# Seven stretches of a graph layer's gathers take 114 to 126 rows in place of 128

## The chip, the cores and the metric

The kernel runs on one core of one Trainium2 chip. The time is device microseconds of that core. Before the change it is 18006.2 us, the median of two runs (18000.0 and 18012.4).

## The reference, cut to what matters

A graph layer over 50,000 nodes with 160 features (64 scalars and 32 vectors of three) and 1,650,000 edges: 800,000 random pairs in both directions and a loop at each node, sorted by destination. Every edge takes its source node's features, combines them with its own four attributes, and the results are summed at the destination. Then come a linear map, a relu, two residual additions and a layer norm.

```python
dst = jnp.concatenate([_d, _s, _loop])
_o = jnp.argsort(dst, stable=True)
src, dst = src[_o], dst[_o]
...
ss, vv = (s[src], v[src])                       # gather per edge
dot = jnp.einsum('eui,ei->eu', vv, e1)
out0 = C0 * (ss * e0 @ W1 + dot * INV3 @ W2)
...                                             # p3, p4, p5 -> out1
m_agg = jax.ops.segment_sum(m, dst, num_segments=n)
h = ...                                         # m_agg times Ws and Wv
return x + jax.nn.relu(h)
...
x = _layernorm(x + ref(x, ...), axis=-1)
```

Everything up to the relu is linear in the source features, so the kernel sums first and multiplies by the weights afterwards: per node, for each of the four attributes, the sum over its edges of attribute times source row.

## The kernel before, in words

Edges are taken in the order of their destination. 128 of them, one per partition, make a unit; six units (G) make a group, twenty groups (SG) a chunk of 120 units. A group's 768 edges reach few nodes, so its sums fit a window of 32 node slots (W).

For a unit, POOL issues one indirect DMA (L398) that fetches 128 rows of x, 640 bytes each, into a slice of the tile `xg`. A tile holds two groups (PG), so twelve gathers, and there are four such tiles; a gather into a tile waits until the matmuls on its earlier contents are done. DVE builds the other operand: `hot` (L419) marks each edge's node slot, and `ha` (L422) multiplies the marks with the four attributes, giving 128 columns (4 attributes times 32 slots). PE multiplies `ha` with the gathered rows (L447) and sums a group's six units in PSUM; each matmul waits for its own gather's semaphore. DVE then transposes the sums (L462) and adds them into a ring of nodes (L471), at a position read from the data. When a block of 128 nodes is complete, PE multiplies it with the weights (L776), and DVE and ACT do the residual and norm (L184 to L200).

Loops of nodes aren't gathered: after a head of the first 100 groups (five chunks), which reads the inputs as they are, rows of edges are packed by DVE and stored to memory without the loops (`edges`, L683), 11 times 128 rows of 1185 edges, and the later chunks read these. The nodes' own rows come in through `xr`. A chunk's edges are loaded by SP (L267, and L273 for the first node of each group) and turned so that edge and unit change places.

The order of work on SP, PE, DVE and ACT is written out by hand: a loop over pairs of groups issues the gathers of a pair, its matmuls, and between these in small portions whatever is due (packing steps, blocks, loads). A chunk's load is asked for three pairs before the chunk ahead of it starts (LEAD), and turned one to two pairs after that start.

## Time and profile before

| | before |
|---|---|
| median of the runs | 18006.2 us |
| the profiled execution | 18022.0 us |
| its span | 18020.3 us |
| POOL busy | 11866.1 us (66%), 12,522 gathers among 12,535 instructions |
| DVE busy | 7478.3 us (41%) |
| PE busy, weight loads | 6860.2 us (38%), 6095.4 us (34%) |
| DMA | 1341.6 MB, mean 74 GB/s |
| TensorE clock granted | 0.627 |

Busy time is that of instructions as the profiler recorded them; for a gather on POOL it is the time in which the engine makes the transfer ready, not the transfer. Idle time is counted just before the instruction that follows it, with what ended it as far as semaphore events show. "issue" means that the engine waited for nothing that the profile shows, and "remote" that the releaser isn't known. q0 is the queue of the gathers, q1 that of SP.

### The profile page before, as it was taken

Reading aid. Unit: us, or ns where it says so; the run is one execution under the profiler, and the core shown is the slowest. Engines: PE = TensorE matmul, PEld = TensorE weight load, DVE = VectorE, ACT = ScalarE, POOL = GpSimd, SP = SyncE. Lnnn points to the kernel's source line nnn. Section 1 sums busy time; section 2 is a strip of 40 time slices with the busy share of each in tenths; the row PEclk is TensorE's granted clock in tenths of the full one; section 3 lists DMA queues with packets and bytes.
Section 4 is the critical chain, followed back from the end, with each engine's and each line's share of the span. In section 5 each row is a group of like instructions: output and inputs, shape, how many; then the busy total and the mean of one; then the engine's idle time right before and its main releaser. Section 6 shows DMA issues by size and latency. Waiting matters only on the chain. (4 is left out here: it accounts for less than half of the span.)

```text
span 18020.3 us, 93561 instructions
## 1 busy us (share of the span) xinstructions
PE 6860.2 (38%) x28971; PEld 6095.4 (34%) x28972; DVE 7478.3 (41%) x12038; ACT 171.6 (1%) x273; POOL 11866.1 (66%) x12535
## 2 busy tenths in 40 slices
PE   3333334333333333333333333333333333333433
PEld 2233333333333333333333333333333333333333
DVE  7344245334524442453344345434433452444232
ACT  0000000000000000000000000000000000000000
POOL 6566666666666666666666666666666666666666
PEclk6666666666666666666666666666666666666666
DMA  2222322322332233223223322332232233222222
GB/s 72 79 71 78 79 68 73 83 76 70 77 81 70 71 80 77 70 73 85 73 70 78 80 70 72 82 77 69 72 85 74 69 76 78 72 70 71 75 72 61
DMA packets 740962, 1341.57 MB, mean 74 GB/s; under 512 B 243310, under 2 KB 522674, under 8 KB 725894
## 3 DMA queue, kind: packets, MB, share of 16 engines
q0 software_dynamic: 601056, 1026.60, 23.5%
q1 hardware_dynamic: 138138, 308.06, 5.6%
q8 instruction: 231, 3.78, 0.1%
q14 instruction: 273, 2.24, 0.0%
q10 hardware_dynamic: 1264, 0.88, 0.0%
HBM read 1263.28 MB, written 71.42 MB: 74 GB/s over the span
## 5 line engine op out<-in xcount | busy, mean ns | idle before, releaser
L398 POOL DMA_INDIRECT xg<-in_x,si x12522 | 11862.6, 947 | 6108.8 <-issue 3663.5
L447 PE MATMUL ps<-xg,ha 128*128 128x160 f32 x25044 | 6282.8, 397 | 9643.7 <-issue 5600.4
L447 PEld LDWEIGHTS ps<-xg,ha 128*128 128x128 f32 x25044 | 5409.4, 267 | 10356.9 <-issue 10352.3
L462 DVE STREAM_TRANSPOSE sums<-ps 128x320 f32<-128x320 f32 x1044 | 527.0, 505 | 6249.8 <-remote 4712.4
L422 DVE TENSOR_TENSOR ha<-hot,pk 128x1536 f32<-128x1536 f32 x1044 | 1830.4, 1753 | 52.1 <-remote 11.0
L776 PE MATMUL phb<-BWk,ring 128*128 128x160 f32 (+1 forms) x3910 | 1176.4, 381 | 1441.0 <-issue 858.6
L184 DVE SCALAR_TENSOR_TENSOR y<-phb,xt 128x320 f32<-128x320 f32 x196 | 95.9, 489 | 3623.2 <-PE ps L447 2504.7
L776 PEld LDWEIGHTS phb<-BWk,ring 128*128 128x128 f32 (+1 forms) x3910 | 894.1, 258 | 1489.1 <-issue 886.9
L471 DVE TENSOR_TENSOR ring<-ring,sums 128x160 f32 x2087 | 684.5, 328 | 253.1 <-issue 158.6
L419 DVE TENSOR_TENSOR hot<-bank,rel 128x384 f32<-128x384 f32 x1044 | 570.6, 547 | 67.4 <-DMA xt<-in_x 67.3
L632 DVE COPY_PREDICATED prow<-marks,prow 128x2370 f32<-128x2370 int32 (+5 forms) x198 | 550.3, 2780 | 1.1
L766 DVE STREAM_TRANSPOSE ring<-xr 128x1280 f32<-128x1280 f32 x188 | 437.2, 2326 | 0.1
L632 DVE COPY_PREDICATED pra<-marks,pra 128x1580 f32<-128x1580 int32 (+5 forms) x198 | 378.8, 1913 | 0.0
L763 DVE TENSOR_TENSOR xr<-xr,bank 128x1280 f32<-128x1280 f32 x188 | 276.5, 1471 | 4.6 <-DVE bank L756 1.4
L194 ACT ACTIVATE rstd<-mv,eps_t 128x2 f32<-128x2 f32 x196 | 58.0, 296 | 16997.5 <-DVE mv L189 12612.7
L468 DVE TENSOR_TENSOR ring<-ring 128x196 f32<-128x196 f32 (+20 forms) x485 | 149.4, 374 | 1.8
L200 DVE TENSOR_SCALAR o<-y,mv,rstd 128x160 f32<-128x160 f32 x391 | 130.2, 374 | 10.9 <-remote 1.6
L629 DVE COPY_PREDICATED_SCALAR hit<-marks,none 128x395 int32 (+5 forms) x198 | 130.1, 657 | 10.9 <-DVE pri L627 3.2
L716 DVE MEMSET ring<- 128x1280 f32 (+1 forms) x98 | 119.3, 1218 | 23.1 <-issue 21.0
L188 DVE BATCH_NORM_STATS2 st<-y 128x6 f32<-128x160 f32 x391 | 121.7, 311 | 6.7
L630 DVE COPY_PREDICATED hit<-marks,pri 128x395 int32<-128x395 int32 (+5 forms) x198 | 118.5, 598 | 10.4 <-issue 2.2
L627 DVE TENSOR_TENSOR pri<-hit,marks 128x395 int32<-128x395 int32 (+11 forms) x198 | 113.5, 573 | 14.8 <-issue 3.2
(346 smaller groups left out, 1752.7 us busy)
## 6 DMA issues: line engine op xcount, KB each, us to landing
xg<-in_x,si POOLq DMA_INDIRECT x12522
xr<-in_x SPq DMA_DIRECT2D x93, 1280.0 KB
r<-edges SPq DMA_DIRECT2D x100, 384.0 KB
edges<-prow SPq DMA_DIRECT2D x1330, 27.8 KB
xt<-in_x SPq DMA_DIRECT2D x195, 160.0 KB
out<-o SPq DMA_DIRECT2D x195, 160.0 KB
pra<-in_attr SPq DMA_DIRECT2D x10, 2370.0 KB
selves<-mine SPq DMA_DIRECT2D x1328, 0.8 KB
```

Of the source, the lines that this page charges most:

```text
L200: nc.vector.tensor_scalar(o[:n, i], y[:n, i], mv[:n, i, 0:1], rstd[:n, i:i + 1], op0=ALU.subtract, op1=ALU.mult)
L398: part = nc.gpsimd.indirect_dma_start(out=xg[:, j, :], out_offset=None, in_=x, in_offset=bass.IndirectOffsetOnAxis(ap=placed[0][:, u + j:u ...
L419: idle[:] = [nc.vector.tensor_tensor(hot[:, :n], slotsP[:, 0:W].unsqueeze(1).to_broadcast([P, n, W]), rel[:, u:u + n].unsqueeze(2).to_broa ...
L422: nc.vector.tensor_tensor(ha[:, :n], hot[:, :n].unsqueeze(2).to_broadcast([P, n, NK, W]), pk[:, :, u:u + n].rearrange("p k u -> p u k").un ...
L447: mm = nc.tensor.matmul(ps[:, j // G, :], ha[:, j].rearrange("p k w -> p (k w)"), xr, start=j % G == 0, stop=j % G == G - 1)
L462: nc.vector.transpose(at[:, :ng], ps[:, :ng].rearrange("p g (b f) -> p g b f", f=FB))
L468: nc.vector.tensor_tensor(ring[k][:, b, :past], ring[k][:, b, :past], ring[k - 1][:, b, S:S + past], op=ALU.add)
L471: nc.vector.tensor_tensor(here, here, at[:, i], op=ALU.add)
L632: nc.vector.copy_predicated(what[:n, a:e], mi[:, r].unsqueeze(2).to_broadcast([n, e - a, what.shape[2]]), what[:n, a + d:e + d])
L763: nc.vector.tensor_tensor(xr[:, r], xr[:, r], sumP[:, r].unsqueeze(2).to_broadcast([P, r.stop - q, D]), op=ALU.mult)
L766: nc.vector.transpose(here[:, r], xr[:, r].rearrange("p q (b f) -> p q b f", f=FB))
L776: wrote("misc", nc.tensor.matmul(ph[:nb], ring[k][:, i, cols], BWk[:, i, :], start=i == 0, stop=i == ND - 1))
```

## The change

In seven stretches of eight chunks the gathers take fewer than 128 rows: 126 in chunks 8 to 15, 125 in 20 to 27, 124 in 32 to 39, 121 in 44 to 51, 119 in 56 to 63, 114 in 68 to 75 and 120 in 80 to 87. Between these and at the end stand chunks of 128, and the chunks before them, the head among them, are as they were. A unit then holds that many edges, on the first partitions; the operands of the matmul are cut to these partitions. With fewer edges in a unit there are more units: the number of groups goes from 2087 to 2146. What stands at which edge is now read from a list of starts, and the loads of a short chunk are split in two, one for the first 96 partitions (whole blocks of 32) and one for the last 32.

```diff
+SIZES = (126, 125, 124, 121, 119, 114, 120)
+
+def size_of(s):
+    i, j = divmod(s - 8, 12)
+    return SIZES[i] if 0 <= i < len(SIZES) and j < 8 else P
...
-    ngroups = math.ceil((n_edges - n_nodes + eh * n_nodes / n_edges + far) / (group * P))
+    starts = [0]
+    while starts[-1] < n_edges - n_nodes + eh * n_nodes / n_edges + far:
+        g = len(starts) - 1
+        starts.append(starts[-1] + group * (P if g < head else size_of(g // SG)))
...
     def near(g):
-        p = g * G * P
+        p = starts[g]
...
+                if size[s] < P:
+                    m = size[s] // W
+                    for i, what_ in ((slice(0, m), what[0:P * size[s] * c]), (slice(m, NK), what[m * W * c:])):
+                        by_unit = what_.rearrange("(u q) -> u q", u=P)[:, 0:(i.stop - i.start) * W * c]
+                        dq.dma_start(to[i.start * W:i.stop * W], by_unit.rearrange("u (i q) -> i u q", q=W * c))
+                    return
...
-            nc.vector.tensor_reduce(extremes[:, 0, s:s + 1], rel[:, :n], axis=AX.X, op=ALU.min)
+            nc.vector.tensor_reduce(extremes[:size[s], 0, s:s + 1], rel[:size[s], :n], axis=AX.X, op=ALU.min)
...
                 part = nc.gpsimd.indirect_dma_start(
-                    out=xg[:, j, :], out_offset=None, in_=x,
-                    in_offset=bass.IndirectOffsetOnAxis(ap=placed[0][:, u + j:u + j + 1], axis=0))
+                    out=xg[:size[s], j, :], out_offset=None, in_=x,
+                    in_offset=bass.IndirectOffsetOnAxis(ap=placed[0][:size[s], u + j:u + j + 1], axis=0))
...
-                mm = nc.tensor.matmul(ps[:, j // G, :], ha[:, j].rearrange("p k w -> p (k w)"), xr,
+                mm = nc.tensor.matmul(ps[:, j // G, :], ha[:xr.shape[0], j].rearrange("p k w -> p (k w)"), xr,
```

Also, `extremes` is set to zero once, and the list of places at which the program changes its margin for a group's first node (`cuts`) has the starts and ends of the stretches added.

The instructions of POOL, before, from the last ones ahead of the main loop to its end (`xg` are the gathered rows, the first number of a shape is the rows of one gather, and xN says how many stand in a row):

```order
L803 IOTA quarter 128x4
L999 IOTA place 128x1185
L398 DMA xg<-in_x,si 128x160 x49
L505 IOTA at 1x1408
L398 DMA xg<-in_x,si 128x160 x12473
L885 TENSOR_LOAD more
```

The same place now, from the same gathers to the stretch of 114 (the line of the gather is now L420):

```order
L420 DMA xg<-in_x,si 128x160 x911
L420 DMA xg<-in_x,si 126x160 x960
L420 DMA xg<-in_x,si 128x160 x480
L420 DMA xg<-in_x,si 125x160 x960
L420 DMA xg<-in_x,si 128x160 x480
L420 DMA xg<-in_x,si 124x160 x960
L420 DMA xg<-in_x,si 128x160 x480
L420 DMA xg<-in_x,si 121x160 x960
L420 DMA xg<-in_x,si 128x160 x480
L420 DMA xg<-in_x,si 119x160 x960
L420 DMA xg<-in_x,si 128x160 x480
L420 DMA xg<-in_x,si 114x160 x960
```

The 49 ahead of `at` are the same; behind these rows stand 480 of 128, 960 of 120 and 2316 of 128. So the queue holds 12,876 gathers, 354 more than before, and 6,720 of them are short.

SP's instructions before, around the load of chunk 8 (`fd` and `r` are a chunk's first nodes and edges, `xt` a block's rows of x, `sa` and `xr` shares and rows of the nodes themselves, `out` the result):

```order
L709 DMA xt<-in_x 128x320
L875 DMA out<-o 128x320
L273 DMA fd<-edges 128x1x1
L267 DMA r_4696<-edges 128x2x384
L709 DMA xt<-in_x 128x320
L746 DMA sa<-selves 128x1x64
L746 DMA xr<-in_x 128x1x2560
```

And now:

```order
L731 DMA xt<-in_x 128x320
L897 DMA out<-o 128x320
L295 DMA fd<-edges 128x1x1
L286 DMA r_4697<-edges 96x4x192
L286 DMA r_4697<-edges 32x4x192
L731 DMA xt<-in_x 128x320
L768 DMA sa<-selves 128x1x64
L768 DMA xr<-in_x 128x1x2560
```

One load has become two, with the next block's rows and the nodes' own rows behind them.

More of the change, by code (lines that the diff above doesn't have):

```diff
@@ L100, in plan @@
     rows = math.ceil((n_edges - eh) / row) + 2
-    ngroups = math.ceil((n_edges - n_nodes + eh * n_nodes / n_edges + far) / (group * P))
-    assert eh + (rows - 1) * row - n_nodes + eh * n_nodes / n_edges - far >= ngroups * group * P
+    starts = [0]
+    while starts[-1] < n_edges - n_nodes + eh * n_nodes / n_edges + far:
+        g = len(starts) - 1
+        starts.append(starts[-1] + group * (P if g < head else size_of(g // SG)))
+    assert size_of((len(starts) - 2) // SG) == P and len(starts) - 1 > head + SG
+    assert eh + (rows - 1) * row - n_nodes + eh * n_nodes / n_edges - far >= starts[-1]
     units = P * math.ceil(max(math.ceil(n_edges / P) + again - 1, math.ceil((eh + rows * row + 1) / P)) / P)
-    return nblk, nb, again, group, units, ngroups, row, head, rows, far
+    return nblk, nb, again, group, units, starts, row, head, rows, far
 @with_exitstack
@@ L110, in tile_gnn_resnorm @@
     N = x.shape[0]
-    NBLK, NB, GA, G, NU, NG, L, NH, NR, FAR = plan(N, n_edges)
+    NBLK, NB, GA, G, NU, starts, L, NH, NR, FAR = plan(N, n_edges)
+    NG = len(starts) - 1
     EH = NH * G * P
@@ L212, in tile_gnn_resnorm @@
     S = SB * P
-    cuts = sorted({0, NH, NG} | {round(i * NG / 10 / SG) * SG for i in range(10)})
+    cuts = sorted({0, NH, NG} | {round(i * NG / 10 / SG) * SG for i in range(10)}
+                  | {g for g in range(NH, NG, SG) if size_of(g // SG) != size_of(g // SG - 1)})
     parts = list(zip(cuts, cuts[1:]))
@@ L219, in tile_gnn_resnorm @@
     NSC = math.ceil(NG / SG)
+    size = [P if s * SG < NH else size_of(s) for s in range(NSC)]
     part_of = [next(i for i, (g0, g1) in enumerate(parts) if g0 <= s * SG < g1) for s in range(NSC)]
@@ L243, in tile_gnn_resnorm @@
         extremes = once.tile([P, 2, NSC], F32, name="extremes")
+        nc.vector.memset(extremes, 0.0)
         count_ = once.tile([1, SG], F32, name="count")
@@ L279, in load @@
                     at = (at[0], g0 - f0, ng)
-                p0, q0 = u0 * P - EH, f0 * G * P - EH
+                p0, q0 = (starts[g0] - EH + (u - g0 * G) * size[s] for u in (u0, f0 * G))
                 r6 = rawp.tile([P, NK * W * C], F32, name="r6").rearrange("p (b e c) -> p b e c", b=NK, c=C)
                 fd = rawp.tile([P, 1], F32, name="fd")
-                fetch_first(fd, edges[0, q0 * C + 1:(q0 + W * G * P) * C + 1], C)
-                fetch(r6.rearrange("p b e c -> p b (e c)"), edges[0, p0 * C:(p0 + P * P) * C], C)
+                fetch_first(fd, edges[0, q0 * C + 1:(q0 + W * G * size[s]) * C + 1], C)
+                fetch(r6.rearrange("p b e c -> p b (e c)"), edges[0, p0 * C:(p0 + P * size[s] + size[s] % P // W * W) * C], C)
                 return s, at, None, None, fd, r6[:, :, :, 0:2].rearrange("p b e c -> p c b e"), r6[:, :, :, 2:]
@@ L382, in place @@
                 op0=ALU.min, op1=ALU.subtract)
-            nc.vector.tensor_reduce(extremes[:, 0, s:s + 1], rel[:, :n], axis=AX.X, op=ALU.min)
-            begun.append(nc.vector.tensor_reduce(extremes[:, 1, s:s + 1], rel[:, :n], axis=AX.X, op=ALU.max))
+            nc.vector.tensor_reduce(extremes[:size[s], 0, s:s + 1], rel[:size[s], :n], axis=AX.X, op=ALU.min)
+            begun.append(nc.vector.tensor_reduce(extremes[:size[s], 1, s:s + 1], rel[:size[s], :n], axis=AX.X, op=ALU.max))
             placed[s] = si, rel, pk[:, :, us]
@@ L405, in gather @@
                 tc.add_to_no_dep_group(key, part.ins)
-                rows.append((xg[:, j, :], filled[t][j], 16 * gathers[t][j], key))
+                rows.append((xg[:size[s], j, :], filled[t][j], 16 * gathers[t][j], key))
             return rows
@@ L918, in reach @@
         def reach(s):
-            end = min(NG, (s + 1) * SG) * G * P
+            end = starts[min(NG, (s + 1) * SG)]
             if s * SG < NH:
@@ L923, in reach @@
             if s + 1 < NSC:
-                end = max(end, (s * SG * G + P) * P)
+                end = max(end, starts[s * SG] + P * size[s] + size[s] % P // W * W)
             if s * SG == NH:
-                end = max(end, (s * SG + W) * G * P)
+                end = max(end, starts[s * SG] + W * G * size[s])
             return end - EH
```

## The prediction

> **What bounds the kernel now.** I read the page first, by engines, queues and groups.

> ```profile
> span 18020.3 us, 93561 instructions
> PE 6860.2 (38%) x28971; PEld 6095.4 (34%) x28972; DVE 7478.3 (41%) x12038; ACT 171.6 (1%) x273; POOL 11866.1 (66%) x12535
> q0 software_dynamic: 601056, 1026.60, 23.5%
> q1 hardware_dynamic: 138138, 308.06, 5.6%
> L398 POOL DMA_INDIRECT xg<-in_x,si x12522 | 11862.6, 947 | 6108.8 <-issue 3663.5
> ```

> No engine is full. But the 12,522 gathers of L398 fill POOL end to end: 11862.6 us busy and 6108.8 us idle just before them make 17971.4 us, so 48.9 us of the span is left for everything else. One gather's slot is 17971.4 / 12522 = 1.435 us, and the time of this kernel is the number of gathers times their slot. The slot has three parts: 0.947 us busy, an issue gap, and waits. The view of waits splits the last two.

> ```profile
> POOL xg L398 <- issue: 3663.5, 12020, 1.7
> POOL xg L398 <- PE ps L447: 1220.3, 220, 33.2
> POOL xg L398 <- remote: 1201.7, 275, 6.9
> PE ps L447 <- issue: 5600.4, 2943, 24.0
> PE ps L447 <- DVE ha L422: 3280.4, 462, 61.0
> ```

> The issue gap is 3663.5 / 12020 = 0.305 us. The rest, 6108.8 - 3663.5 = 2445.3 us, is 0.195 us a gather, and stands in some 500 waits of several us. The timeline of POOL shows how they fall (these are its rows with a wait, from one answer):

> ```profile
> 5135.98 0.95 POOL L398 DMA_INDIRECT xg<-in_x,si  x1 [6.50 <-PE ps L447]
> 5170.51 0.94 POOL L398 DMA_INDIRECT xg<-in_x,si  x1 [4.74 <-PE ps L447]
> 5204.95 0.94 POOL L398 DMA_INDIRECT xg<-in_x,si  x1 [4.59 <-remote]
> 5239.69 0.94 POOL L398 DMA_INDIRECT xg<-in_x,si  x1 [5.03 <-remote]
> ```

> These waits are 34.5 us apart, which is 24 gathers (two tiles of twelve): 24 x 1.25 us of gathering and about 4.6 us of waiting for one of the four xg buffers, which PE's matmuls hand back. So POOL can issue at 1.25 us, and something downstream holds it to 1.435. The timeline of all engines up to the second of these waits shows PE then:

> ```profile
> 5164.82 0.94 POOL L398 DMA_INDIRECT xg<-in_x,si  x1 [0.30 <-issue]
> 5165.12 0.43 PE L447 MATMUL ps<-xg,ha 128*128 128x160 f32 x1 [2.37 <-issue]
> 5166.52 0.28 PEld L447 LDWEIGHTS ps<-xg,ha 128*128 128x128 f32 x1 [2.50 <-issue]
> 5167.92 0.42 PE L447 MATMUL ps<-xg,ha 128*128 128x160 f32 x1 [2.37 <-issue]
> 5170.02 1.30 PEld L447 LDWEIGHTS ps<-xg,ha 128*128 128x128 f32 x5 [1.12 <-issue]
> 5170.03 1.43 PE L447 MATMUL ps<-xg,ha 128*128 128x160 f32 x4 [0.27 <-issue]
> ```

> While gathers stream, PE gets one instruction every 1.40 us (5165.12, 5166.52, 5167.92) with no releaser that the profile names; some 4 us after POOL has stopped it runs four matmuls in 1.43 us. So gathers in flight slow PE, PE hands buffers back late, POOL waits, and that lets PE catch up. What in a gather does this (its 128 rows, its completion on the DMA engines, or its being one instruction) the trace doesn't show, since all its gathers are alike. It does show what it is not: the pace hardly moves with other traffic. Two stretches of the windows view (busy time of the gathers' own tile, granted clock, DMA share, GB/s):

> ```profile
> 5400.00:5850.00 450.00, 162.97 (x625) 139.21 (x626) 297.24 (x314) 0.63 0.28 70
> 13050.00:13500.00 450.00, 159.21 (x644) 137.29 (x644) 293.75 (x312) 0.62 0.32 84
> ```

> At 70 and at 84 GB/s POOL gets 314 and 312 gathers through in 450 us.

> **The change part by part.** The base is the profiled execution, 18022.0 us: its span and 1.7 us around it. It is 15.8 us (0.1%) over the median of the two timed runs, 18006.2; sums are made against 18022.0.

> More gathers. By the order of POOL there are 49 + 911 + 7 x 960 + 6 x 480 + 2316 = 12876 gathers, 354 more. The 6720 short ones lack 960 x (2 + 3 + 4 + 7 + 9 + 14 + 8) = 45120 rows in all, 6.71 a gather, and the other 6156 keep 128. At the slot of before the extra ones cost 354 x 1.435 = 508 us. That is the upper end of the plain case: 18530.

> Shorter gathers. No row of the trace has a gather of another length, so what a missing row saves lies between nothing and its full share of the slot, 1435 / 128 = 11.2 ns. At the full share the 45120 rows give back 506 us and the total is 18024. [...] 45120 x 7.4 = 334 us, so the sum is 18022 + 508 - 334 = 18196. A gain beyond the full share, or a loss beyond 508, needs another mechanism; both stand under the rivals.

> [...]

> Matmuls over fewer rows. L447 sums over 114 to 126 partitions in place of 128; the tile shapes that PE streams (160 columns) stay, so I cost it at nothing. The trace's 397 ns a pass times the 2 x 354 added passes is 281 us on an engine that is 38% busy; PE's part in the slot is priced in the wait already. The cover would be gone if PE were full.

> ```profile
> L447 PE MATMUL ps<-xg,ha 128*128 128x160 f32 x25044 | 6282.8, 397 | 9643.7 <-issue 5600.4
> L422 DVE TENSOR_TENSOR ha<-hot,pk 128x1536 f32<-128x1536 f32 x1044 | 1830.4, 1753 | 52.1 <-remote 11.0
> L419 DVE TENSOR_TENSOR hot<-bank,rel 128x384 f32<-128x384 f32 x1044 | 570.6, 547 | 67.4 <-DMA xt<-in_x 67.3
> ```

> DVE work for 59 more groups. 29.5 pairs of hot and ha, 2.3 us each, are 68 us on an engine that is 41% busy. It would come out only where PE waits for ha, and that wait goes with the pairs: part of the slot again.

> Loads of a chunk. In 56 chunks the one load of edges becomes two on SP's queue, one more issue each.

> ```profile
> 5350.80 0.69 SPq L267 DMA_DIRECT2D r<-edges  x1
> 5463.92 0.58 SPq L273 DMA_DIRECT2D fd<-edges  x1
> ```

> An added issue holds SP some 0.6 us; behind it stand the x rows of later blocks, asked for two pairs (34 us) ahead, so nothing waits. A chunk's edges are asked for three pairs before the chunk ahead of it begins, and read two pairs into that one: five pairs, 86 us. Nothing. Without that cover it is 56 x 0.6 = 34 us. The memset of extremes and the narrower reductions are DVE work under 1 us.

> **The rivals.** (1) The slot belongs to the gather, not to its rows: POOL's shorter busy time only makes it wait longer for its buffers, since what holds PE back comes once a gather. For it: POOL already waits 0.195 us a gather, so what it saves isn't on the path while PE sets the pace; the pace didn't move between 70 and 84 GB/s. Against it: POOL's own 1.25 us is most of the slot. Time 18530, 2.8% over.

> (2) Fewer engines per gather lighten it. A gather of 128 rows leaves 601056 / 12522 = 48 packets, 16 times 3, so each of the 16 DMA engines takes part alike. If short ones go out on fewer engines and with fewer packets, and these are what slows PE, the wait of 0.195 us goes: 6720 x 0.195 = 1310 us, and 18530 - 1310 = 17220. It decides if PE keeps its fast pace while POOL streams. Against it: other queues' packets come and go without moving the pace, so packets as such are hardly the cause.

> (3) Fewer engines per gather make it longer. Suppose that a gather's rows are split evenly, over the largest number of engines up to 16 that divides them: 128 rows give 16 engines with 8 rows each (as the 48 packets have it), and 126, 125, 124, 121, 119, 114 and 120 give 14, 5, 4, 11, 7, 6 and 15, with 9, 25, 31, 11, 17, 19 and 8 rows on each. [...] q0 takes 23.5% of 16 engines, 0.235 x 16 x 18020 / 12522 = 5.4 us of engine time a gather. If 124 rows always went to the same four engines, that is 5.4 x 124 / 128 / 4 = 1.31 us on each, and with their share of q1 (5.6 / 23.5 x 5.4 / 4 = 0.32) 1.63 us against the slot of 1.435; the other lengths stay below it. That adds 960 x 0.2 = 190 us to rival 1: 18720. [...]

> That the change doesn't do what it says I leave out: the order shows the lengths.

> **How the numbers follow.** Forecast (rows save busy time): 0.42, own range 18020 to 18360. Rival 1: 0.26. Rival 2: 0.19. Rival 3: 0.13, half of it mild. A measurement here can tell about 2% from no change, 360 us. So faster by over 2% is 0.19 (rival 2), within 2% is 0.42 (forecast), slower 0.39 (rivals 1 and 3). The time is that of the likeliest, 18196 less the profiled run's 15.8: 18180. The range goes from rival 2 to the mild side of rival 3, 17200 to 18800; only the heavy side of rival 3 is left out.

> **What would show it.** The gathers of L420 by their lengths: busy about 947 - 7.4 ns for each missing row (932 at 126, 843 at 114) and a count of 12876. If busy stays at 947 or the waits grow by what it loses, and the slot stays 1.435 us in every stretch, rival 1 holds. Where a stretch runs near 1.25 us a gather without the waits of several us, rival 2. Where the stretches of 124 and 125 rows are far slower than those of 126 and 120, rival 3. A slot that differs between stretches by more than their lengths explain makes the forecast wrong, whatever the sum.

## The result: slower by 4.0%, in two of the seven stretches and in the count

| | before | after |
|---|---|---|
| median of the runs | 18006.22 us (18000.04 to 18012.40) | 18733.11 us (18732.84 to 18733.39) |
| ratio | | 1.0404, 95% interval 1.0359 to 1.0448 |
| the profiled execution | 18022.0 us | 18732.8 us |
| granted TensorE clock | 0.627 | 0.602 |

The forecast was 18180 us. The time lies inside its range, 553 us over the forecast itself. The page of the changed kernel, by engines, queues and the group of the gathers:

```profile
span 18731.1 us, 95746 instructions
PE 7919.1 (42%) x29679; PEld 6424.2 (34%) x29680; DVE 7601.3 (41%) x12228; ACT 171.4 (1%) x273; POOL 13203.0 (70%) x12889
q0 software_dynamic: 725568, 1030.86, 22.8%
q1 hardware_dynamic: 154490, 309.25, 5.5%
L420 POOL DMA_INDIRECT xg<-in_x,si x12876 | 13199.5, 1025 | 5483.3 <-issue 3787.9
```

The gathers are still the whole span: 13199.5 us busy and 5483.3 us idle ahead of them are 18682.8 of 18731.1 us. There are 12,876, as counted. But their mean busy time went up, from 947 to 1025 ns, although they fetch fewer rows; and what POOL waits beside its issue gap went down, from 2445 to 5483.3 - 3787.9 = 1695 us.

The windows view, for the gathers' tile alone, takes the stretches apart. The columns are the window, its length, then busy time and number of instructions of PE, of its weight loads and of POOL, then granted clock, DMA share and GB/s. The eight windows lie inside the stretches of 126, 125, 124, 121, 119, 114 and 120 rows and inside the last stretch, of 128:

```profile
1500.00:2800.00 1300.00, 448.74 (x1815) 378.83 (x1813) 889.95 (x907) 0.63 0.29 75
3550.00:4900.00 1350.00, 728.90 (x1816) 432.85 (x1816) 1075.70 (x901) 0.54 0.29 69
5700.00:7100.00 1400.00, 720.55 (x1760) 424.17 (x1760) 1131.87 (x881) 0.53 0.29 68
7850.00:9150.00 1300.00, 475.32 (x1838) 403.55 (x1838) 913.45 (x905) 0.61 0.27 72
9950.00:11250.00 1300.00, 506.30 (x1808) 402.93 (x1807) 990.58 (x910) 0.59 0.28 71
12000.00:13300.00 1300.00, 610.05 (x1856) 426.43 (x1855) 1013.40 (x909) 0.58 0.28 71
14050.00:15350.00 1300.00, 453.69 (x1832) 390.31 (x1833) 895.69 (x911) 0.62 0.28 69
15500.00:18600.00 3100.00, 1076.06 (x4344) 926.55 (x4344) 2056.26 (x2169) 0.62 0.29 73
```

A window's length over POOL's count is the slot, POOL's busy time over its count is a gather's busy time. The packets of q0 in the same windows show how a gather's rows are split. They hold seven rows at most (4480 bytes): at 126 rows a gather has 14 packets of 4480 bytes and 14 of 1280, so fourteen shares of nine rows; at 125 it has 15 of 4480 and 5 of 2560, so five of 25; at 124 16 of 4480 and 4 of 1920; at 121 11 and 11 of 2560; at 119 14 and 7 of 1920; at 114 12 and 6 of 3200; at 120 15 and 15 of 640; at 128 16 and 16 of 640. The page counts 16 engines, and a gather has sixteen shares when those without rows (below) are counted. So I take a share for the part of one engine, as the expectations do; the packet records name no engine. Ordered by the rows of the largest share:

| rows | shares x rows in each | busy, us | busy + 0.305 | slot, us |
|---|---|---|---|---|
| 128 | 16 x 8 | 0.948 | 1.253 | 1.429 |
| 120 | 15 x 8 | 0.983 | 1.288 | 1.427 |
| 126 | 14 x 9 | 0.981 | 1.286 | 1.433 |
| 121 | 11 x 11 | 1.009 | 1.314 | 1.436 |
| 119 | 7 x 17 | 1.089 | 1.394 | 1.429 |
| 114 | 6 x 19 | 1.115 | 1.420 | 1.430 |
| 125 | 5 x 25 | 1.194 | 1.499 | 1.498 |
| 124 | 4 x 31 | 1.285 | 1.590 | 1.589 |

Two things are to be seen. Busy time follows the last factor of the second column, not the first column: 114 rows take longer to issue than 128. And the slot stays at 1.43 us until busy time and the issue gap of 0.305 us together pass it; from there the slot is that sum, to 0.001 us. So the surplus adds up from its parts: 354 gathers x 1.435 = 508 us, plus 960 x (1.498 - 1.435) = 60 and 960 x (1.589 - 1.435) = 148, together 716 us. The profiled executions differ by 18732.8 - 18022.0 = 711.

In the stretch of 124, PE behaves differently. The timeline of the changed kernel there:

```profile
6499.72 1.29 POOL L420 DMA_INDIRECT xg<-in_x,si  x1 [0.30 <-issue]
6500.51 0.50 PEld L469 LDWEIGHTS ps<-xg,ha 124*128 124x128 f32 x2 [0.98 <-DMA xg<-in_x,si]
6500.51 0.90 PE L469 MATMUL ps<-xg,ha 124*128 124x160 f32 x2 [0.58 <-DMA xg<-in_x,si]
6501.31 1.28 POOL L420 DMA_INDIRECT xg<-in_x,si  x1 [0.30 <-issue]
6502.15 0.50 PEld L469 LDWEIGHTS ps<-xg,ha 124*128 124x128 f32 x2 [1.14 <-DMA xg<-in_x,si]
6502.15 0.90 PE L469 MATMUL ps<-xg,ha 124*128 124x160 f32 x2 [0.74 <-DMA xg<-in_x,si]
```

Each gather's two matmuls run together, released by its landing, and POOL hardly waits for a buffer (9.7 us in the window's 1400). Nothing is left of the single instructions 1.40 us apart that the prediction quotes from before. The view of waits has it for the whole kernel, first before and then after (us in total, times, longest):

```profile
PE ps L447 <- DMA xg<-in_x,si: 1.0, 2, 0.6
```

```profile
PE ps L469 <- DMA xg<-in_x,si: 1508.8, 1760, 10.4
POOL xg L420 <- PE ps L469: 947.2, 259, 30.5
```

PE waits for a landing by name 1,760 times, near the 1,920 gathers of 125 and 124 rows, and before it all but never did. Such counts depend on which updates of semaphores the trace has on record: in the window of 126 rows it holds 2,948 that came from transfers, where the gathers alone make 907 x 16 = 14,512; in the window of 124 rows it holds 14,651, where they make 14,096. The trace's records of q0's packets don't have these gaps, and they say the same. From the last of a gather's 16 completions (its 16 packets of 4 bytes, as many as it adds to its semaphore) to PE's first matmul on its rows, the median is 31.1 us in the window of 126 rows and 0.5 us in that of 124.

### The profile page after: what moved, and what is told of

Read it like the earlier page. It is cut to its first block, busy times and chain, and to the rows that moved or that the text cites. A ratio compares the mean times of both kernels' runs of the same rounds, so it can differ in the third digit from the quotient of the medians.

```text
span 18731.1 us, 95746 instructions
## 1 busy us (share of the span) xinstructions
PE 7919.1 (42%) x29679; PEld 6424.2 (34%) x29680; DVE 7601.3 (41%) x12228; ACT 171.4 (1%) x273; POOL 13203.0 (70%) x12889
## 3 DMA queue, kind: packets, MB, share of 16 engines
q0 software_dynamic: 725568, 1030.86, 22.8%
## 5 line engine op out<-in xcount | busy, mean ns | idle before, releaser
L420 POOL DMA_INDIRECT xg<-in_x,si x12876 | 13199.5, 1025 | 5483.3 <-issue 3787.9
L469 PE MATMUL ps<-xg,ha 128*128 128x160 f32 (+7 forms) x25752 | 7302.0, 421 | 9639.9 <-issue 4808.6
L469 PEld LDWEIGHTS ps<-xg,ha 128*128 128x128 f32 (+7 forms) x25752 | 5696.7, 273 | 11072.8 <-issue 8769.3
L444 DVE TENSOR_TENSOR ha<-hot,pk 128x1536 f32<-128x1536 f32 x1073 | 1881.4, 1753 | 59.9 <-issue 10.8
L490 DVE TENSOR_TENSOR ring<-ring 128x133 f32<-128x133 f32 (+40 forms) x485 | 148.4, 372 | 2.3 <-issue 0.4
```

The source lines that it names most:

```text
L420: part = nc.gpsimd.indirect_dma_start(out=xg[:size[s], j, :], out_offset=None, in_=x, in_offset=bass.IndirectOffsetOnAxis(ap=placed[0][:si ...
L444: nc.vector.tensor_tensor(ha[:, :n], hot[:, :n].unsqueeze(2).to_broadcast([P, n, NK, W]), pk[:, :, u:u + n].rearrange("p k u -> p u k").un ...
L469: mm = nc.tensor.matmul(ps[:, j // G, :], ha[:xr.shape[0], j].rearrange("p k w -> p (k w)"), xr, start=j % G == 0, stop=j % G == G - 1)
L490: nc.vector.tensor_tensor(ring[k][:, b, :past], ring[k][:, b, :past], ring[k - 1][:, b, S:S + past], op=ALU.add)
```

## The experiments

The theory after the result, called A in the expectations: a gather has a floor of some 1.43 us, whatever its rows and engines; POOL's busy time rises with the rows of the largest share (0.948 us at 8, 1.285 at 31); the slot is the larger of the floor and POOL's own time. The first three runs change only the table of sizes. Where no range or interval stands beside a time, it is that of one or two executions; thirteen executions of the kernel before lay within 0.13% of each other.

### Without the stretches of 125 and 124

```diff
-SIZES = (126, 125, 124, 121, 119, 114, 120)
+SIZES = (126, 128, 128, 121, 119, 114, 120)
```

> The changed kernel with 128 rows in place of 125 and of 124 in its second and third stretch (126, 121, 119, 114 and 120 stay): 12,822 gathers, 300 more than the kernel before. Theory A (a gather has a floor of 1.43 us, whatever its rows and engines, and only where POOL's own busy time plus its 0.305 us gap is over that does POOL set the pace): 300 x 1.435 = 431 us over the kernel before, about 18437 us; every remaining short stretch runs at 1.43 us a gather, with waits. Rival B (short gathers on few engines cost wherever they stand, so the surplus over the count is spread over all seven stretches): the whole shrinks only with the count, 18733 x 12822 / 12876 = 18654 us, and stretches of 114 and 119 come out over 1.43 us.

Measured 18446.96 us (18444.76 to 18454.77), 1.0246 times the kernel before (interval 1.0229 to 1.0263). A said 18437, B 18654. The windows of the two places that now have 128 rows:

```profile
3500.00:4900.00 1400.00, 474.33 (x1929) 409.67 (x1928) 930.31 (x980) 0.62 0.28 73
5500.00:6900.00 1400.00, 487.38 (x1955) 420.11 (x1954) 929.09 (x979) 0.63 0.27 75
```

Both are back at 1.43 us (1400 / 980). Of the surplus of 727 us between the medians, 286 us went with two lengths out of seven: 54 gathers fewer (77 us) and about 209 us of POOL's own time. What remains, 441 us, is the count (300 x 1.435 = 430) to 11 us. So five of seven lengths cost nothing but their extra gathers.

### Whole sixteens, down to 64 rows

```diff
-SIZES = (126, 125, 124, 121, 119, 114, 120)
+SIZES = (112, 96, 80, 64, 88, 72, 128)
```

> The changed kernel with stretches of 112, 96, 80, 64, 88, 72 and 128 rows: 14,442 gathers, 1,920 more than before. The first four lengths are multiples of 16 (16 engines with 7, 6, 5 and 4 rows each), 88 and 72 are 11 engines x 8 and 12 x 6. Theory A: the floor of 1.43 us holds down to 64 rows, 18006 + 1920 x 1.435 = 20760 us, while busy falls by some 13.5 ns for each row fewer per engine (0.935, 0.92, 0.91, 0.89 us), so the waits grow; 88 has about 0.98 us busy, with a surplus of some 35 ns because it is not on 16 engines. Rival C (the forecast's step: busy goes by rows at 7.4 ns each, and the slot with it): 64 rows are busy 0.47 us in a slot of 0.96 us, and the total is 20760 - 245760 x 0.0074 = 18940 us.

Measured 20731.72 us; A said 20760, C 18940. Windows of 112, 96, 80, 64, 88 and 72 rows:

```profile
1500.00:2800.00 1300.00, 447.41 (x1838) 385.92 (x1836) 842.84 (x912) 0.61 0.25 69
3550.00:4850.00 1300.00, 455.01 (x1833) 399.21 (x1833) 830.88 (x912) 0.59 0.22 59
5600.00:6900.00 1300.00, 525.34 (x1817) 467.69 (x1817) 818.51 (x909) 0.52 0.19 52
7650.00:8950.00 1300.00, 557.35 (x1843) 487.73 (x1842) 823.41 (x914) 0.50 0.17 43
9700.00:11000.00 1300.00, 531.38 (x1862) 464.69 (x1862) 886.34 (x910) 0.53 0.21 56
11750.00:13050.00 1300.00, 528.60 (x1812) 468.80 (x1812) 855.22 (x911) 0.52 0.17 47
```

At 64 rows a slot is 1300 / 914 = 1.422 us. Half the rows and 43 in place of some 75 GB/s save less than 1% of it, although busy time fell to 0.901 us and PE ran at a granted clock of 0.50. Rows aren't in the floor, nor are bytes. Busy time is 0.924, 0.911, 0.900 and 0.901 us at 7, 6, 5 and 4 rows a share: the step between neighbours shrinks to nothing (A had a steady 13.5 ns a row, down to 0.89). 88 rows in 11 shares (8 in each) take 0.974 us and 72 in 12 (6 in each) 0.939, 27 and 28 ns more than the same number of rows in each of 16 shares (0.947 and 0.911).

### Rows in one, two and three shares

```diff
-SIZES = (126, 125, 124, 121, 119, 114, 120)
+SIZES = (127, 123, 122, 117, 110, 105, 104)
```

> The changed kernel with stretches of 127, 123, 122, 117, 110, 105 and 104 rows: 13,182 gathers, 660 more than before. By the largest divisor up to 16 these go to 1, 3, 2, 13, 11, 15 and 13 engines with 127, 41, 61, 9, 10, 7 and 8 rows on each. Theory A (POOL writes as many entries for every engine as the fullest has rows, 0.84 us + 13.5 ns a row): busy 2.59 us at 127, 1.43 at 123, 1.70 at 122; slots 2.90, 1.73 and 2.00 us, the other four stretches at 1.43 us; total 18006 + 660 x 1.435 + 960 x (1.465 + 0.295 + 0.565) = 21185 us. Rival D (the transfer on the few engines sets the pace, all gathers on the same ones: 5.4 us of engine time a gather): 5.4 us a gather at 127, 2.6 at 122, 1.7 at 123, about 24000 us in all, with POOL waiting for buffers in these stretches.

Measured 21153.12 us; A said 21185, D about 24000. Windows of 127, 123, 122 and 117 rows, and the row of the gathers' queue:

```profile
1500.00:4200.00 2700.00, 835.61 (x1861) 465.63 (x1861) 2365.17 (x930) 0.50 0.21 40
5000.00:6500.00 1500.00, 733.06 (x1752) 425.90 (x1752) 1233.33 (x876) 0.52 0.26 60
7300.00:9100.00 1800.00, 783.97 (x1828) 456.85 (x1828) 1521.60 (x915) 0.51 0.25 54
9850.00:11150.00 1300.00, 470.50 (x1809) 397.99 (x1809) 890.21 (x906) 0.61 0.26 70
q0 software_dynamic: 1047456, 1039.70, 20.1%
```

At 127, 123 and 122 rows slots are 2.903, 1.712 and 1.967 us, busy times 2.543, 1.408 and 1.663. At 123 and 122 rows the slot is again the busy time and 0.304 us. At 127 rows the difference is 0.360 us: most gathers there too follow each other after 0.30 us, but ten times in these 2700 us POOL stands for 1.8 to 9.9 us, each time at a place where PE waits 11 to 17 us for a landing. So landings came late at these ten places, with all rows in one share; what delayed them no run shows. From 61 to 127 rows in a share busy time grows by 0.880 us, 13.3 ns a row; from 31 (the 124 rows of the changed kernel, 1.285 us) to 61 by 0.378, 12.6 ns a row. But for those ten places the transfer is not the bound even with one share: gathers follow each other at POOL's pace, and the packets with rows (4480 and 640 bytes), whose times add up to 3915 us in this window of 2700, overlap.

The bytes of q0 show what few shares bring with them. The rows are 1,602,816 x 640 bytes = 1025.80 MB, and sixteen completions of 4 bytes for 13,182 gathers 0.84 MB. That leaves 13.06 MB. If every share without rows, up to sixteen, has 4 bytes for each row that the others hold, the lengths have 15 x 127 + 13 x 41 + 14 x 61 + 3 x 9 + 5 x 10 + 1 x 7 + 3 x 8 = 3400 such entries, and 3400 x 960 x 4 bytes = 13.06 MB. The same count for the changed kernel (18 + 275 + 372 + 55 + 153 + 190 + 8 = 1071) gives 4.11 MB, and its q0 moved 1030.86 - 1025.93 - 0.82 = 4.11. The packets show it too: in the changed kernel's window of 124 rows (881 gathers) q0 has 14,075 packets of 4480 bytes and 3,520 of 1920, which makes 16 and 4 a gather (seven and three rows each, so four shares of 31 rows), and 42,192 of 28 bytes and 10,548 of 12, which makes 48 and 12 (seven and three times 4 bytes, so twelve shares of 31 entries). Counted so, 124 rows make 16 x 31 = 496 rows and entries, 128 rows 16 x 8 = 128. Busy time grows with the same number, by 13 ns for each row more in the largest share; what POOL does in that time no run shows.

### What the floor of 1.43 us is not

The next runs change the kernel before, all of whose gathers have 128 rows. First, fewer waits on PE:

```diff
-                gathers[t][j] += 1
+                gathers[t][j // G] += 1
...
-                part.then_inc(filled[t][j], 16)
+                part.then_inc(filled[t][j // G], 16)
...
-                mm.wait_op(sem, count, "sem-ge")
+                if j % G == 0:
+                    mm.wait_op(sem, count, "sem-ge")
```

> The kernel before, with one semaphore for the six gathers of a group (counted to 96) in place of six counted to 16; PE waits once a group, at its first matmul. Gathers, matmuls and results are the same. Theory S (something behind POOL serves one gather in 1.43 us, and PE only shows it): no change, 18006 us, slot 1.435. Rival P (PE's own waits, one for each gather, hold it back while gathers stream): PE keeps up, POOL's waits for buffers of 0.195 us a gather go, 18006 - 12522 x 0.195 = 15560 us, or part of that way.

Measured 17991.23 us against 18008.2, ratio 0.9992 (0.9982 to 1.0002): no change. Rival P is out.

Half of PE's work:

```diff
-                gathers[t][j] += 1
+                gathers[t][j // 2] += 1
...
+                if j % 2 == 0:
+                    yield ps
+                    continue
                 mm = nc.tensor.matmul(ps[:, j // G, :], ha[:, j].rearrange("p k w -> p (k w)"), xr,
-                                      start=j % G == 0, stop=j % G == G - 1)
+                                      start=j % G == 1, stop=j % G == G - 1)
```

> The kernel before, with a semaphore for every two gathers and a matmul only for the second of them: half of the 25,044 passes and weight loads, and half of the products, are left out (so the sums lack every second unit). All gathers are made and waited for. Theory S (something behind POOL serves one gather in 1.43 us): no change, 18006 us. Rival P2 (PE gets its instructions slowly while gathers stream, and it is their number that holds the buffers): with half of them PE keeps up, POOL's 0.195 us a gather of waits go, 15560 us.

Measured 17853.24 us against 17995.22, 0.8% less; P2 asked for nearly 14%. With half the passes the slot is 1.42 us:

```profile
PE 4498.8 (25%) x16449; PEld 3878.8 (22%) x16450; DVE 7468.3 (42%) x12038; ACT 171.4 (1%) x273; POOL 11873.1 (67%) x12535
L398 POOL DMA_INDIRECT xg<-in_x,si x12522 | 11869.6, 948 | 5953.3 <-issue 3703.6
```

(11869.6 + 5953.3) / 12522 = 1.423 us. With half as many instructions PE keeps POOL waiting nearly as long, so PE's passes show the floor and don't make it. What the 0.8% are, no run tells.

Three buffers in place of four:

```diff
-            tc.tile_pool(name="idx", bufs=2) as idxp, tc.tile_pool(name="rows", bufs=4) as rowp, \
+            tc.tile_pool(name="idx", bufs=2) as idxp, tc.tile_pool(name="rows", bufs=3) as rowp, \
...
-            t = begun_tiles[0] % 4
+            t = begun_tiles[0] % 3
```

> The kernel before, with three xg buffers in place of four. Theory S (a server at 1.43 us a gather behind POOL): the mean slot stays 1.435 us, 18006 us, since a shorter queue in front of the same server only makes POOL wait more often and less long each time. Rival J (the waits come from unevenness that four buffers don't even out): fewer buffers, more waiting; with the 0.195 us of waits going up by a third or more, 18006 + 12522 x 0.065 = 18820 us or above.

Measured 18004.66 us against 17995.22, 0.05% more. The waits for buffers are not unevenness that a deeper queue would even out.

More completions, from another queue:

```diff
             for j in range(n):
+                if j % 2:
+                    more = extrap.tile([16, 4], F32, name="more")
+                    nc.sync.dma_start(more, x[0:16, 0:4])
                 part = nc.gpsimd.indirect_dma_start(
```

The second run of this pair loads 17 partitions in place of 16.

> The kernel before, with one more small load on SP's queue for every two gathers (16 partitions of 16 bytes, so one descriptor and one completion on each of 16 engines), into a tile that nothing reads: 6,261 loads. Theory S1 (completions are served one after another, 1.43 / 16 = 89 ns each, whoever sends them): 16 more for two gathers, the slot goes to 1.5 x 1.43, about 27000 us. Theory S2 (the floor belongs to the gathers' own queue or to POOL): no change, 18006 us, since the loads move 1.6 MB in all and SP's queue takes 5.5% of the engines.

> As the run on 16 engines, but each added load has 17 partitions, which go to one engine (17 is prime) with 17 descriptors and one completion on it. Theory S1: one completion more for two gathers, slot 1.435 + 0.045 us, 18570 us. Theory S2: 18006 us. If instead every issue of SP costs the gathers something, this run and the one on 16 engines come out alike.

Measured 18060.19 and 18066.93 us against 17995.22. S1 asked for 27000 and 18570. SP's queue shows the loads (first the run on 16 engines, then that on one; the kernel before has 138138 packets):

```profile
q1 hardware_dynamic: 338490, 310.07, 6.5%
```

```profile
q1 hardware_dynamic: 250836, 309.79, 6.2%
```

The 200,352 added packets are 6,261 x 32, 16 rows and 16 completions each, and the 112,698 are 6,261 x 18, 17 rows and one completion. The bytes agree: 16 x 16 + 16 x 4 = 320 a load make 2.00 MB of the 2.01 added to 308.06, and 17 x 16 + 4 = 276 make the 1.73. Both runs cost 0.4%, alike, so what little they cost doesn't go with completions: 100,000 more of them from another queue left the slot at 1.44 us.

Then POOL's own time. A memset behind each gather was to add 0.1 or 0.3 us to POOL alone:

```diff
+        spare = once.tile([1, 1], F32, name="spare")
...
                 rows.append((xg[:, j, :], filled[t][j], 16 * gathers[t][j], key))
+                nc.gpsimd.memset(spare, 0.0)
```

> The kernel before, with one memset of a single number on POOL behind every gather (12,522 more instructions; the page of before has memsets of 96 to 117 ns). Theory S (the floor is behind POOL, which has 1.435 - 1.25 = 0.18 us to spare in each slot): the memset takes that spare time, POOL's waits shrink by what it adds, and the time stays at 18006 us within 0.5%. Rival Q (POOL's own instruction stream sets the slot, its waits being a part of how it works through gathers): 12522 x 0.10 to 0.13 us more, 19260 to 19630 us.

> As the run with one memset, with three behind every gather. Theory S with POOL as the second bound: POOL's own time goes to 1.25 + 3 x 0.1 = 1.55 us or, with gaps, 1.65; that is over 1.43, so its waits for buffers vanish and the slot is that time: 19400 to 20700 us, as in the stretches of 125 and 124 rows, here with 128 rows on 16 engines. Rival E (those stretches were slow for their rows and engines and not for POOL's time): the waits stay and the time is 18006 + 12522 x 0.3 = 21760 us, or it does not move at all.

Measured 19705.79 and 23166.35 us against 18010.0. That looks like Q, but these two runs don't test it: POOL's order was left to the scheduler here, and it had put the memsets together in front of most gathers. The timeline of the run with three, in a place where the kernel before gathers:

```profile
5130.04 0.09 POOL L408 MEMSET spare<- 1x1 f32 x1
5130.19 0.09 POOL L409 MEMSET spare<- 1x1 f32 x1
5130.33 0.09 POOL L407 MEMSET spare<- 1x1 f32 x1
5130.48 0.09 POOL L408 MEMSET spare<- 1x1 f32 x1
```

No gather lies beside them, so their time adds: 12522 x 0.147 = 1841 us for one, against 1696 measured. The two runs were made again with POOL held to the order of the program:

```diff
-        later_pools.enter_context(tc.manual_schedule(engines={ET.SP, ET.PE, ET.DVE, ET.Activation}))
+        later_pools.enter_context(tc.manual_schedule(engines={ET.SP, ET.PE, ET.DVE, ET.Activation, ET.Pool}))
```

> The kernel before, with one memset of a single number on POOL behind every gather, and POOL too held to the order of the program (in the two runs with memsets before this one they had all been moved together, ahead of the main loop's gathers, and their time simply added). A memset takes 0.089 us and 0.059 us ahead of it, 1116.1 + 736.9 us for 12,522. Theory S (a floor of 1.43 us a gather behind POOL, and 0.18 us of slack in POOL itself): POOL's own time goes to 1.25 + 0.147 = 1.40 us, still under the floor, so the time stays at 18006 us within 1%, and the waits shrink to 0.03 us a gather. Rival Q (POOL's time adds to the slot whatever it waits): 12522 x 0.14 = 1750 us more, 19760 us.

> As the run with one memset between gathers, with three. Theory S with POOL as the second bound: POOL's own time is 1.25 + 3 x 0.147 = 1.69 us, over the floor, so there are no waits for buffers left and the total is 12522 x 1.69 + 49 = 21210 us; PE and SP get through their instructions as in the stretches of 125 and 124 rows, with no gaps of 1.4 us between them. Rival Q: 18006 + 3 x 1750 = 23260 us, with the waits of 0.195 us a gather as they were.

With one memset 18087.97 us against 18048.35, ratio 1.0023 (1.0012 to 1.0034): it costs nearly nothing, as S said. It did so in another way than I had reckoned. The timeline of this run:

```profile
9000.64 0.94 POOL L399 DMA_INDIRECT xg<-in_x,si  x1 [3.05 <-remote]
9001.59 0.09 POOL L407 MEMSET spare<- 1x1 f32 x1
9001.89 0.95 POOL L399 DMA_INDIRECT xg<-in_x,si  x1 [0.22 <-issue]
```

The memset sits in the gap between two gathers, which are still 1.25 us apart. So this run shows that POOL's gap has room for 0.09 us, and not that its waits give way.

With three memsets 18805.26 us, 4.2% over 18048.35: far from Q's 23260, and below the 21210 of S, since here too the gap took up a part of them. Its rows:

```profile
L399 POOL DMA_INDIRECT xg<-in_x,si x12522 | 11860.0, 947 | 2125.3 <-issue 663.0
4000.00:8000.00 4000.00, 2208.32 (x5337) 1289.69 (x5337) 2526.59 (x2669) 0.54 0.28 71
PE ps L451 <- DMA xg<-in_x,si: 7176.6, 9422, 8.9
POOL xg L399 <- PE ps L451: 17.1, 30, 0.9
```

(The page's row of the gathers, the windows view of their tile, and the view of waits.) The slot is 4000 / 2669 = 1.499 us. This is the stretch of 125 rows over again, with 128 rows in 16 shares: with POOL's own time over 1.43 us its waits for buffers are gone (17.1 us in all, where before had 1220.3 and 1201.7 more without a known releaser), and PE waits for landings by name, 9,422 times. So POOL's time alone is enough to make such a stretch; how the rows of those two stretches were split mattered through POOL's time.

What the floor is made of stays open. It is not the rows or bytes (64 to 128 rows), not the number of shares with rows (6 to 16), not PE's waits or passes, not the buffers, and not completions that another queue adds.

The packets of q0 show that it isn't the transfers either. In the kernel before, a gather's first packet starts 0.7 us and the last of its 16 completions ends 1.3 us after POOL is done with it (medians; 99% of the completions within 5.9 us), and over a burst of 24 gathers at 1.25 us it doesn't fall further behind (medians of 1.30 to 1.35 us from its first gathers to its last). PE's first matmul on these rows starts 34 us later still (median), in the run with three memsets held between gathers 0.39 us later. So what comes late lies behind the landing. One place in the run with half the passes shows it: by the trace, twelve passes of PE ended at 5152.7 us, and DVE, which was idle, took up their sums 16 us later, while POOL stood still (5162.4 to 5168.87). PE went on after that, with rows that had all landed by 5149.1:

```profile
5168.63 0.52 DVE L467 STREAM_TRANSPOSE sums<-ps 128x320 f32<-128x320 f32 x1 [19.64 <-remote]
5174.23 1.14 PE L452 MATMUL ps<-xg,ha 128*128 128x160 f32 x3 [21.55 <-issue]
```

The handing over from engine to engine was late here. What holds it up while POOL gathers every 1.25 us, and no longer at 1.50, no run here tells. Three things were the same in all runs: each gather's own 16 completions, DVE's work for each gather (DVE is 41% busy), and the recording of the execution. Since the trace lacks most updates of semaphores in the stretches at the floor (2,948 of 14,512 at 126 rows), and hardly any at 124 rows, the recording may have a part in the floor; that is a guess.

## Why the prediction was wrong

**What bounds the kernel now.** Right: the time is the number of gathers times their slot, and something downstream holds POOL from 1.25 to 1.435 us. "PE gets one instruction every 1.40 us" was right as a reading, and it was right to leave its cause open; half of PE's passes left the floor where it was. The packets of before show besides that the rows had landed long before PE took them up.

**More gathers.** Right: 12,876, and 508 us. This term alone is 1.0282 times the base, and with five short lengths (the first experiment) the measured ratio is 1.0246 for 300 extra gathers.

**Shorter gathers.** This is the step that failed. The sum takes 45120 x 7.4 = 334 us off, 7.4 ns being 947 / 128; no run shows such a term, and in its place the runs show a busy time that goes by the largest share, in a slot that doesn't follow it below 1.43 us. So two things are wrong with it, and either would have been enough.

First, busy time doesn't go by rows. It goes by the rows of the largest share: in 6 shares 114 rows take 1.115 us where I had 0.843. The term was forecast at -334 us and is +208 (960 x (0.063 + 0.154)), and only two lengths make it.

Second, and plainer, POOL's busy time was not on the path. Where it did fall, the waits grew by it: at 64 rows 1.422 - 0.901 - 0.305 = 0.216 us a gather, at 128 rows in the changed kernel 1.429 - 0.948 - 0.305 = 0.176. The prediction had the reason in its own words, under rival 1: "POOL already waits 0.195 us a gather, so what it saves isn't on the path while PE sets the pace". With 0.195 us of waits in every slot nothing that POOL saved came through, down to 0.901 us busy at 64 rows; the forecast contradicted the reading ahead of it, and its 0.42 should have stood with rival 1.

**Rival 1** (the slot belongs to the gather, 18530) held wherever POOL's own time stayed under 1.43 us: in five of the seven stretches, and down to 64 rows. Without 125 and 124 it is right to 0.1% (18437 expected by its rule, 18447 measured).

Shorter gathers saved nothing while the largest share had 4 to 19 rows (0.90 to 1.12 us busy, slots of 1.42 to 1.44); at 25 rows a share and more POOL's part was the bound. In the kernel before a gather takes 0.947 + 1.32 = 2.27 us from its start on POOL to its last completion, so POOL's part of it is not small.

**Rival 2** (fewer engines lighten a gather, 17220) didn't occur. The stretches without waits are the slow ones (slots of 1.498 and 1.589 us): the waits vanished because POOL became slower, not because PE became faster.

**Rival 3** (fewer engines make a gather longer) had the place right and the price wrong. "Where the stretches of 124 and 125 rows are far slower than those of 126 and 120, rival 3": they are slower, by 0.16 and 0.07 us. Its mild side priced the transfer on four fixed engines (1.63 us at 124, against 1.589 measured, and nothing at 125, against 1.498). That it came near at 124, and with its total of 18720, is chance: by the same sum 127 rows on one engine would need 5.4 us a gather, and the slot there was 2.903. The heavy side, which the range left out, would be all of the busy time growing with the rows of the largest share. That dependence is right and the size wrong: from 0.947 us at 8 rows it would have gone to 2.96 at 25, and 1.194 was measured. Only about 13 ns a row is added (12.6 to 13.3 by the slopes above); from 8 rows on, the line through these points leaves some 0.84 us that doesn't grow with the rows (at 4 and 5 rows busy time stays at 0.90). With that split and the 0.03 us more that were measured where not all 16 shares have rows, 0.87 + 0.013 x 25 = 1.195 and 0.87 + 0.013 x 31 = 1.27 us, against 1.194 and 1.285 measured, and the two slow stretches follow from their shares.

The split itself, which rival 3 supposed (the largest divisor of the rows up to 16), fits q0 in all 21 lengths from 64 to 128: the packets of the changed kernel's windows above, and the whole of q0 in the runs with other lengths (616,416 packets and 1026.97 MB from 112 down to 64 rows, 1,047,456 and 1039.70 MB from 127 to 104, just what packets of up to seven rows in such shares make). The busy times fit it too (0.900 to 2.543 us by the rows of a share).

**What I costed at nothing** was nothing, to 5 us: the passes over fewer rows (0.247 us busy a pass at 126 rows and 0.248 at 120 and 128, by the windows), DVE's 29 more pairs, the 56 loads made in two. The parts above add to 716 us, and 711 were measured.

## What to carry to other kernels

Before a saving on an engine is priced, look whether that engine waits in every round: if it does, as here, its saving can be worth nothing (0.901 us busy at 64 rows, a slot of 1.422), and its growth nothing either, up to the slot (1.115 us busy at 114 rows, a slot of 1.430); past that point the slot here was busy time and 0.305 us (1.498 at 125 rows, 1.589 at 124). For gathers as these, take as many rows as fit, in a number that the packets show split into small shares (128 rows in 16 shares have 8 each; up to 19 in each stayed at the floor), since a gather cost about 1.43 us here whether it brought 64 rows or 128. 127 rows, all in one share, were the worst, at 2.90 us.
